# A second batch of column copies in every second step, a tenth row fetch, and column sides loaded slot by slot

## The chip, the cores and the metric

The kernel runs on one core of a Trainium2 chip. The core has a tensor engine (PE, with its weight loads shown as PEld), a vector engine (DVE), a scalar engine (ACT), GpSimd (POOL), and SyncE (SP), which here only issues transfers. Each engine works through its own queue of instructions in order; semaphores make one engine wait for another or for a transfer. A queue also holds register loads, register arithmetic and the issuing of DMAs, which the profile does not count as busy time of the engine.

The metric is the time of one execution on the device in microseconds (us). The kernel before took 1935.29 us, the median of six runs from 1933.59 to 1936.26.

## The reference, cut to what matters

One layer of a graph network over 12500 nodes of 64 features and 200000 edges, which are sorted by their target node, and a layer norm at the end. All of it is float32.

```python
nodes = x[edges].reshape(E, -1)                          # source row and target row of each edge
gates = ssp(edge_attr @ We1 + be1) @ We2 + be2           # ssp(v) = softplus(v) - log 2
gates = gates * (1 - sigmoid(5 * (distance - 3.5)))
h = ssp(nodes @ Wn1 + bn1) @ Wn2 + bn2
sums = zeros_like(x).at[dst].add(h * gates)
new = x + (ssp(sums @ Ws1 + bs1) @ Ws2 + bs2)
out = layernorm(x + new)
```

The source rows `x[src]` are in random order. 

## The kernel before, in words

**Steps and chunks.** The edges are cut into 391 steps of 512 edges, and each step into four chunks of 128. Every chunk needs the source rows of its 128 edges. Since the edges are sorted by target, the targets of 256 edges lie within 42 consecutive nodes, so the target side is not gathered: a table `x @ Wn1[64:] + bn1`, made in the preparation, is read in windows of 42 rows (line 313) and multiplied with a one-hot matrix of the targets (line 342).

**Three ways for the source rows.** 
- GpSimd gathers a chunk with one indirect DMA (line 258), 14 steps ahead of its use. This is the usual way.
- A few chunks, the "row slots", are fetched row by row on ACT's queue: `read_rows` (line 272) loads eight row addresses into registers with one register load, and `fetch` (line 284) issues one small DMA of 256 bytes per row, `ROWS[1]` = 9 rows per step. `slots_by_rows` gives a slot each time 128 rows have come together. In the step of such a slot, DVE also copies the one-hot columns to the row tile (line 345).
- A few chunks, the "column slots", are copied by DVE from `xh`, a transposed copy of x in SBUF with the two halves of the nodes on the two halves of the partitions. `columns` (lines 319 to 337) loads eight column numbers into registers (line 325) and copies eight columns of 128x1 (line 332), once per step from step 8 on. When 128 columns are together, an instruction at line 336 keeps of each column the half that holds the node, by comparing `sides` (the source numbers, broadcast to all partitions, with a sign by partition) with `border`. PE multiplies the result with `wn1_twice` into z (line 383). `slots_by_columns` gives a slot each time 128 columns have come together, and `gather` leaves these chunks out, with a memset by DVE (line 256) in their place.

**One step of the loop** (line 697 on). The order in each queue is the order of the program text; no scheduler changes it. PE: transposes of the gathered chunks (L356), first-layer biases (L368, L407), the scatter of an older step (L436), the edge part of layer 1 (L373), the node part (L380, L383), layer 2 of the step before (L414, L419). ACT: copy of the transposed rows (xT, L363), the register load (L272), three row fetches (L284), exp (L394), three fetches, the logarithm (L397), three fetches. DVE: register load of two window bases (L444), two additions into `sums` (L453), h and msg (L428, L432), softplus (L402), the one-hot matrix of a later step (L342), and the batch of columns (L325, L332). SP: loads of edge features (L305) and windows of the table (L313), five steps ahead.

**Node blocks.** When all edges of 512 nodes are done, a block of the last part (the second network and the layer norm) is spread over the following steps. There are 25 blocks. Low node numbers have more edges, so the first blocks come about 40 steps apart and the last ones 8.

**Preparation.** The first 80 us bring in the inputs, make the table and the register lists. SP loads the sides for all 23 slots in one broadcast of 1.5 MB (line 564), and DVE multiplies them with the sign (line 664).

Of the kernel before, what the change touches and what calls it, by code (L numbers as in the profile page):

```python
# [42 lines left out]
F32 = mybir.dt.float32  # L43
BF16 = mybir.dt.bfloat16
I32 = mybir.dt.int32
U8 = mybir.dt.uint8
AF = mybir.ActivationFunctionType
OP = mybir.AluOpType
# [9 lines left out]
P = 128  # L58
# [14 lines left out]


BLOCK_STEPS = ((2, 3, 4, 4, 6, 7, 8, 9, 10, 14), (2, 3, 3, 4, 5, 6, 7, 8, 9, 10), (1, 2, 1, 2, 3))
ROWS = (0, 9)
READ = 8
ROWS_FROM = -1
READY = (5, 7)
# [1 line left out]
COLUMNS = 8  # L81
COLUMNS_FROM = 8
# [39 lines left out]
def slots_by_columns(NG):  # L122

    slots = []
    for g in range(NG - 2):
        if (g - 3 - COLUMNS_FROM + 1) * COLUMNS >= (len(slots) + 1) * P:
            slots.append((g, 1))
    return slots

# [13 lines left out]
def gnn_resnorm_kernel(ctx: ExitStack, tc: tile.TileContext, a: dict, out: bass.AP, E: int):  # L143
    nc = tc.nc
# [59 lines left out]
    half_n = a["xh"].shape[1]  # L204
    by_columns = {slot: n for n, slot in enumerate(slots_by_columns(NG))}
    columns_i = const.tile([P, column_columns(NG)], I32, name="columns_i")
    sides_i = const.tile([P, len(by_columns) * P], I32, name="sides_i")
    sides = sides_i.bitcast(F32)
    sign = const.tile([P, 1], F32, name="sign")
    border = const.tile([P, 1], F32, name="border")  # L210
    wn1_twice = const.tile([P, 2 * D], F32, name="wn1_twice")
# [64 lines left out]
    def fetch(i, queue, count):  # L276

        for _ in range(min(count, rows_left(queue)) if i >= ROWS_FROM else 0):
            n, r = divmod(fetched[queue], P)
            n += firsts[queue]  # L280
            _, g, k = slots[n]
            if r == 0:
                row_tiles[n, "in"], xrs[g, k] = row_tile(queue, n), row_tile(queue, n)
            ins = queues[queue].dma_start(row_tiles[n, "in"][r : r + 1, :D].bitcast(U8),  # L284
                                          x_bytes[:, bass.ds(row_at[queue].pop(0), 4 * D)])
            tc.no_tile_sem_insts.add(ins.ins.name)
            ins.then_inc(arrived(g, k)[0], 16)
            if r == 0:
                behind(ins, ("rows read", n - 2))
            fetched[queue] += 1  # L290
# [23 lines left out]
                wns[D:DW, g % REST, h, :].bitcast(U8),  # L314
                table_bytes[:, bass.ds(bases[g][h], 8 * D * W)].rearrange("o (w f) -> (o w) f", w=W))), old)

    column_tiles, chosen_columns, columns_done = {}, {}, [0]

    def columns(i, pool):

        n = columns_done[0]
        if i < COLUMNS_FROM or n >= len(by_columns) * P:
            return
        p, q = (n // COLUMNS) % P, n // (COLUMNS * P) * COLUMNS
        _, at = nc.values_load_multi_w_load_instructions(  # L325
            columns_i[p : p + 1, q : q + COLUMNS], engines=[DVE], min_val=0, max_val=half_n - 1,
            skip_runtime_bounds_check_because="src holds rows of x")
        slot = list(by_columns)[n // P]
        if n % P == 0:
            column_tiles[slot] = pool.tile([P, P], F32, name="column", bufs=1)  # L330
        for j in range(COLUMNS):
            nc.vector.tensor_copy(column_tiles[slot][:, n % P + j : n % P + j + 1], xh[:, bass.ds(at[j], 1)])  # L332
        columns_done[0] += COLUMNS
        if columns_done[0] % P == 0:
            chosen_columns[slot] = pool.tile([P, P], F32, name="chosen", bufs=1)
            nc.vector.scalar_tensor_tensor(chosen_columns[slot], sides[:, n // P * P : (n // P + 1) * P], border,
                                           column_tiles[slot], OP.is_ge, OP.mult)

    xTs, zs, us, ss, ghs, hs, msgs, scs = ({} for _ in range(8))

# [202 lines left out]
    with tc.manual_schedule():  # L543
# [4 lines left out]
        with tc.tile_pool(name="prep", bufs=1) as prep:  # L548
# [12 lines left out]
                load_x(i)  # L561
            nc.sync.dma_start(rows_i, a["rows"])
            nc.sync.dma_start(columns_i, a["columns"])
            nc.sync.dma_start(sides_i, a["sides"].partition_broadcast(P))
            dist = cut.rearrange("p g k -> p (g k)")
            nc.sync.dma_start(dist, a["dist_l"])
            dst_i = rel.bitcast(I32)
# [78 lines left out]
            for i in range(PARTS):  # L646
                for c in range(i * CP, (i + 1) * CP, CP // 2):
                    m = CP // 2
                    ps = z_tile().rearrange("p b (k f) -> p (b k) f", k=K)
                    for k in range(m):  # L650
                        nc.tensor.matmul(ps[:, k, :], xT[:, c + k, :], wnb, start=True, stop=True)
                    tb = prep.tile([P, m, 2 * D], F32, name="tb", bufs=6)
                    nc.scalar.copy(tb[:, :K, :], ps[:, :K, :])
                    nc.vector.tensor_copy(tb[:, K:, :], ps[:, K:m, :])
                    nc.sync.dma_start(by_node[:, c : c + m], tb)
                    nc.vector.memset(sums[:, c * P : WIDE if c + m == NCH else (c + m) * P], 0.0)
                if i == 1:
                    nc.vector.tensor_copy(base_i[:1], base_b[:1])
                    nc.vector.tensor_scalar(base_i[32:33], base_b[32:33], float(8 * D), None, OP.mult)
                    nc.vector.tensor_scalar(rows_i, rows_i, float(4 * D), None, OP.mult)  # L660
                    upper = prep.tile([P, column_columns(NG)], F32, name="upper")
                    nc.vector.tensor_scalar(upper, columns_i, float(half_n), float(-half_n), OP.is_ge, OP.mult)
                    nc.vector.tensor_tensor(columns_i, columns_i, upper, OP.add)
                    nc.vector.tensor_scalar(sides, sides_i, sign, None, OP.mult)
                    for k in range(2):
                        nc.vector.tensor_copy(be3[:, k, :], rows[:, 0, :])
                    for k in range(K):
                        nc.vector.tensor_copy(row3[:, :, k, :], rows[:, 1:3, :])
                        nc.vector.tensor_copy(rs3[:, k, :], rows[:, 3, :])
                if i == 2:  # L670
                    nc.scalar.activation(dist, dist, AF.Sigmoid, bias=steep, scale=-5.0)
                    nc.scalar.preload_act_table_set("natural_log_exp_and_others")
                    nc.vector.tensor_copy(rel, dst_i)
                    for t in range(2):
                        r = rel[:, :, 2 * t : 2 * t + 2]
                        nc.vector.tensor_sub(r, r, base_b[:, :NH].rearrange("p (g h) -> p g h", h=2))


        with tc.tile_pool(name="finish", bufs=1) as finish:
# [17 lines left out]
            for i in range(-1, last - 1):  # L697
                now = parts.pop(i, [])
                early = [part for part in now if part.tensor]
                at(load, i + LOADS)  # L700
                if 0 <= i < XH_PARTS:
                    part = slice(half_n * i // XH_PARTS, half_n * (i + 1) // XH_PARTS)
                    nc.sync.dma_start(xh[:, part], a["xh"][:, part])
                if i >= 0:
                    at(gather, i + AHEAD)
                transposes(i + 1, ("load", i + 1), ("gather", i + 1), ("onehot", i + 1))
                xcopy(i + 1)
                read_rows(i, 1, ROWS[1])
                fetch(i, 1, ROWS[1] - 6)
                layer1_bias(i + 1)  # L710
                at(layer2_bias, i)
                for n, g in enumerate(behind_by(i)):
                    scatter(g, zs[i + 1][:, 1, HE + 2 * n * W : HE + 2 * (n + 1) * W])
                layer1_edge(i + 1)
                layer1_node(i + 1)
                exps(i + 1)
                fetch(i, 1, 3)
                logs(i + 1)
                fetch(i, 1, 3)
                for g in behind_by(i):  # L720
                    window(g)
                at(layer2, i)
                for part in early:
                    part.tensor(tx_tile())
                at(hcut, i)
                at(message, i)
                softplus(i + 1)
                for part in early:
                    part.others()
                at(onehot, i + 3)  # L730
                columns(i, finish)
                for part in now:
                    if not part.tensor:
                        part.others()
                complete = i
                if blocks and complete >= blocks[0][1] - PREPARE and not begun:
                    begun = node_block(*blocks[0][0], finish)
                    begun.pop(0).others()
                if blocks and complete >= blocks[0][1]:
                    steps = next(steps for steps in BLOCK_STEPS if i + steps[-1] < last - 1)  # L740
                    for n, part in zip(steps, begun):
                        parts.setdefault(i + n, []).append(part)
                    rest = begun[len(steps) :]
                    blocks.pop(0)
                    begun = None
# [202 lines left out]
```

## Time and profile before

| what | value |
|---|---|
| median of six runs | 1935.29 us |
| profiled execution | 1933.19 us, span 1931.4 us |
| granted clock of PE, mean over the span | 0.983 |
| busy share PE / DVE / ACT / POOL | 92% / 67% / 50% / 74% |
| gathers on POOL (L258) | 1514, mean 0.949 us, the last starts at 1901.6 us |
| row fetches on ACT's queue (L284) | 3328 issues, median 0.223 us each |
| register loads for them (L272) | 416, median 0.742 us |
| column copies on DVE (L332) | 2944, mean 0.148 us |
| register loads for them (L325) | 368, median 0.624 us |
| register loads of window bases (L444) | 391, median 0.543 us |
| copies xT, one per step (L363) | 391, from 80.2 to 1906.1 us |

How to read it: a busy share is the time in which the engine computes, or, for POOL, prepares an indirect DMA. The time that a queue spends on register loads (TENSOR_LOAD), register arithmetic (FUSED_REGOPS) or on issuing (lines with ACTq, SPq, DVEq) is not in it, so an engine that is half idle can have a full queue. The releaser behind an arrow is inferred from semaphores: "issue" means that nothing the profile shows was waited for.

### The profile page before, as it was taken

What the parts mean: (1) busy time and instruction counts of PE and PEld (TensorE: products, weight loads), DVE (VectorE), ACT (ScalarE), POOL (GpSimd) and SP (SyncE); (2) the same over time, 40 slices, a digit from 0 to 9 for tenths busy, and PEclk for the clock granted to TensorE, in tenths of its full rate; (3) what the DMA queues carried; (4) which work ended last, traced back from release to release, by engine and by line L of the source; (5) the groups of instructions that cost most, each with busy time, mean ns of one, the idle gap of its engine ahead of it and who ended that gap; (6) DMA issues with size and microseconds to landing.
All of it is one profiled execution on the core that took longest, in us unless ns stands there. A gap on an engine that the chain in (4) does not pass through costs nothing.

```text
span 1931.4 us, 48239 instructions
## 1 busy us (share of the span) xinstructions
PE 1774.8 (92%) x11419; PEld 1454.7 (75%) x11419; DVE 1299.6 (67%) x5743; ACT 964.8 (50%) x1318; POOL 1437.5 (74%) x1518
## 2 busy tenths in 40 slices
PE   4899999999999999998999998999999999999996
PEld 3787887877787777777777777777777777777775
DVE  4367776777776666666667666676766677677664
ACT  1255555555555454544554554545555555555553
POOL 7777777777777777777777777777777777777773
PEclk9999999999999999999999999999999999999997
DMA  8723332323232232223232232322232223233221
GB/s 231 246 72 72 71 71 67 72 66 73 66 74 68 64 70 64 70 65 70 64 70 66 68 70 66 71 69 67 70 71 68 69 70 71 69 73 73 69 66 24
DMA packets 146498, 147.57 MB, mean 76 GB/s; under 512 B 46735, under 2 KB 93371, under 8 KB 146082
## 3 DMA queue, kind: packets, MB, share of 16 engines
q1 hardware_dynamic: 89578, 92.27, 16.5%
q0 software_dynamic: 48448, 49.71, 14.1%
q10 hardware_dynamic: 8184, 2.44, 0.7%
q8 instruction: 97, 1.59, 0.4%
q14 instruction: 191, 1.56, 0.3%
HBM read 134.61 MB, written 9.63 MB: 75 GB/s over the span
## 4 chain that ended last, share of the span: by engine, by line
PE 45%; ACTq 16%; issue 9%; DVE 9%; DMA 8%; ACT 7%; POOL 3%; DVEq 2%; SPq 1%; POOLq 0%
ACTq L284 13%; PE z L380 10%; PE gh L419 7%; PE z L436 6%; PE tx L356 6%; DMA xg<-in_x,src_i 6%; PE z L373 5%; PE gh L414 4%; ACT xT L363 3%; POOL xg L258 3%; ACT u L394 2%; ACTq L272 2%; PE gh L407 2%; DVE h L428 2%; PE z L368 2%
## 5 line engine op out<-in xcount | busy, mean ns | idle before, releaser
L258 POOL DMA_INDIRECT xg<-in_x,src_i x1514 | 1437.3, 949 | 464.8 <-issue 336.7
L394 ACT ACTIVATE u<-z 128x768 f32<-128x768 f32 x392 | 317.4, 810 | 691.3 <-PE z L380 598.0
L453 DVE TENSOR_TENSOR sums<-sums,z 64x42 f32 x778 | 153.0, 197 | 495.6 <-ACT u L394 453.9
L380 PE MATMUL z<-xT,wns 106*128 106x256 f32 x1564 | 422.1, 393 | 8.4 <-ACT xT L363 7.8
L397 ACT ACTIVATE u<-u,one 128x768 f32<-128x768 f32 x392 | 366.1, 934 | 67.8 <-ACT u L394 63.2
L419 PE MATMUL gh<-consts,s 128*128 128x64 f32 x3128 | 394.9, 269 | 0.0
L419 PEld LDWEIGHTS gh<-consts,s 128*128 128x128 f32 x3128 | 384.1, 193 | 0.0
L402 DVE SCALAR_TENSOR_TENSOR s<-u,z 128x768 f32<-128x768 f32 x392 | 369.3, 942 | 12.2 <-ACT u L397 10.3
L380 PEld LDWEIGHTS z<-xT,wns 106*128 106x128 f32 x1564 | 297.7, 195 | 74.6 <-ACT xT L363 28.4
L356 PE MATMUL tx<-consts,xg 128*106 128x128 f32 x1538 | 238.8, 276 | 93.3 <-DVE h L428 27.5
L436 PEld LDWEIGHTS z<-xg,msg 128*128 128x128 f32 x1556 | 204.6, 191 | 123.8 <-issue 121.1
L363 ACT COPY xT<-tx 106x512 f32<-106x512 f32 x391 | 228.2, 584 | 125.8 <-PE tx L356 115.6
L332 DVE COPY column<-xh 128x1 f32 x2944 | 266.5, 148 | 25.7 <-issue 24.5
L436 PE MATMUL z<-xg,msg 128*128 128x84 f32 x1556 | 264.8, 293 | 0.3
L414 PEld LDWEIGHTS gh<-consts,s 128*128 128x128 f32 x1564 | 239.3, 196 | 31.6 <-DVE s L402 11.1
L356 PEld LDWEIGHTS tx<-consts,xg 128*106 128x106 f32 x1538 | 170.6, 139 | 112.6 <-issue 51.8
L373 PE MATMUL z<-eT,consts 128*128 128x256 f32 x782 | 255.1, 409 | 0.0
L414 PE MATMUL gh<-consts,s 128*128 128x128 f32 x1564 | 244.9, 279 | 4.5 <-DVE s L402 3.8
L428 DVE TENSOR_TENSOR h<-gh,cut 128x256 f32<-128x256 f32 x391 | 166.0, 425 | 26.9 <-PE gh L419 13.9
L432 DVE TENSOR_TENSOR msg<-gh,h 128x256 f32<-128x256 f32 x391 | 165.9, 424 | 13.4
L407 PE MATMUL gh<-row,ones 3*128 3x512 bf16 x391 | 146.8, 375 | 0.0
L342 DVE TENSOR_TENSOR xg<-consts,rel 128x168 f32<-128x168 f32 x391 | 128.3, 328 | 0.0
(102 smaller groups left out, 726.2 us busy)
## 6 DMA issues: line engine op xcount, KB each, us to landing
xr<-in_x ACTq DMA_DIRECT2D x3328, 0.2 KB
eT<-in_eT SPq DMA_DIRECT2D x195, 256.0 KB
xg<-in_x,src_i POOLq DMA_INDIRECT x1514
wns<-table SPq DMA_DIRECT2D x782, 21.0 KB
table<-tb SPq DMA_DIRECT2D x14, 448.0 KB
sums<-in_xT SPq DMA_DIRECT2D x7, 455.0 KB
y<-in_x SPq DMA_DIRECT2D x24, 128.0 KB
out<-y SPq DMA_DIRECT2D x24, 128.0 KB
```

Of the source, the lines that this page charges most:

```text
L258: note(("gather", g), nc.gpsimd.indirect_dma_start(out=xg[:, k, :D], out_offset=None, in_=x, in_offset=bass.IndirectOffsetOnAxis(ap=src_i[ ...
L332: nc.vector.tensor_copy(column_tiles[slot][:, n % P + j : n % P + j + 1], xh[:, bass.ds(at[j], 1)])
L356: ins = nc.tensor.transpose(tx[:, k, :], xgs[g][:, k, :DW], ident)
L363: note(("xcopy", g), nc.scalar.copy(xT, xTs[g]))
L373: nc.tensor.matmul(zs[g][:, 0, :HE], we1.rearrange("a h d -> a (h d)"), eTs[g], start=False, stop=True, skip_group_check=True)
L380: nc.tensor.matmul(zn, wns[:, g % REST, h, :], xTs[g][:, h], start=True, stop=not chosen, skip_group_check=True)
L394: nc.scalar.activation(us[g][:, part], z_of(g)[:, part], AF.Exp)
L397: nc.scalar.activation(us[g][:, part], us[g][:, part], AF.Ln, bias=one)
L402: nc.vector.scalar_tensor_tensor(ss[g].rearrange("p i t e -> p (i t e)")[:, part], us[g][:, part], BIG, z_of(g)[:, part], OP.min, OP.max)
L414: nc.tensor.matmul(v[:, 0, t], ss[g][:, 0, t, :], we2, start=False, stop=False, skip_group_check=True)
L419: nc.tensor.matmul(ghs[g][:, 1, 2 * t + h, :], ss[g][:, 1 + h, t, :], wn2, start=False, stop=h == 1 and t == 1, skip_group_check=True)
L436: ins = nc.tensor.matmul(sc, msgs[g][:, 2 * t : 2 * t + 2, :].rearrange("p h f -> p (h f)"), xgs[g][:, 2 * t : 2 * t + 2, D:DW], start=t = ...
```

## The change

- `ROWS` becomes (0, 10): ten rows are fetched per step on ACT's queue. Behind xT there are three as before (`ROWS[1] - 6` is now written 3), behind exp three, and behind the logarithm four.
- `columns` is called twice in steps with an odd number and once in the others. `slots_by_columns` counts one and a half batches per step.
- The sides are no longer loaded and signed in the preparation. At the first column of each slot SP loads the 128 source numbers of that slot, broadcast to 128 partitions. At the slot's end DVE makes a mask from them in one instruction (times sign, compared with border), and multiplies the columns with it in a second one, in place of the one instruction at line 336. The tiles of side, mask and column have one buffer each.

```diff
-ROWS = (0, 9)
+ROWS = (0, 10)
...
     for g in range(NG - 2):
-        if (g - 3 - COLUMNS_FROM + 1) * COLUMNS >= (len(slots) + 1) * P:
+        steps = g - 3 - COLUMNS_FROM + 1
+        if (steps + steps // 2) * COLUMNS >= (len(slots) + 1) * P:
             slots.append((g, 1))
...
-    sides_i = const.tile([P, len(by_columns) * P], I32, name="sides_i")
-    sides = sides_i.bitcast(F32)
...
         if n % P == 0:
             column_tiles[slot] = pool.tile([P, P], F32, name="column", bufs=1)
+            side_tiles[slot] = pool.tile([P, P], I32, name="side", bufs=1)
+            nc.sync.dma_start(side_tiles[slot], a["sides"][n : n + P].partition_broadcast(P))
...
         if columns_done[0] % P == 0:
+            mask = pool.tile([P, P], F32, name="mask", bufs=1)
+            nc.vector.tensor_scalar(mask, side_tiles[slot], sign, border, OP.mult, OP.is_ge)
             chosen_columns[slot] = pool.tile([P, P], F32, name="chosen", bufs=1)
-            nc.vector.scalar_tensor_tensor(chosen_columns[slot], sides[:, n // P * P : (n // P + 1) * P], border,
-                                           column_tiles[slot], OP.is_ge, OP.mult)
+            nc.vector.tensor_mul(chosen_columns[slot], mask, column_tiles[slot])
...
-            nc.sync.dma_start(sides_i, a["sides"].partition_broadcast(P))
...
-                    nc.vector.tensor_scalar(sides, sides_i, sign, None, OP.mult)
...
-                fetch(i, 1, ROWS[1] - 6)
+                fetch(i, 1, 3)
...
                 fetch(i, 1, 3)
                 logs(i + 1)
-                fetch(i, 1, 3)
+                fetch(i, 1, 4)
...
-                columns(i, finish)
+                for _ in range(1 + i % 2):
+                    columns(i, finish)
```

More of the change, by code (lines that the diff above doesn't have):

```diff
@@ L315, in load @@
                 table_bytes[:, bass.ds(bases[g][h], 8 * D * W)].rearrange("o (w f) -> (o w) f", w=W))), old)
-    column_tiles, chosen_columns, columns_done = {}, {}, [0]
+    column_tiles, side_tiles, chosen_columns, columns_done = {}, {}, {}, [0]
     def columns(i, pool):
```

## The prediction

> **What bounds the kernel now.** The profiled execution took 1933.19 us, of which the span is 1931.4, so 1.8 lie outside; the median of the six runs is 1935.29, 2.1 above it. The sums below are made on the span and get these 3.9 us at the end. 0.2% (3.9 us) is about the least change that a measurement of this kernel can tell.
>
> I read the page's busy shares first. PE at 92% looks like the bound, so I asked the waits whether any engine never waits for work, and found GpSimd.
>
> ```profile
> PE 1774.8 (92%) x11419; PEld 1454.7 (75%) x11419; DVE 1299.6 (67%) x5743; ACT 964.8 (50%) x1318; POOL 1437.5 (74%) x1518
> POOL xg L258 <- issue: 336.7, 1104, 0.3
> ```
>
> GpSimd's longest wait under "issue" is 0.3 us. Its timeline shows the same 0.94 us of work and 0.30 us of pause whatever the pause is put down to, also where it names a DMA or PE:
>
> ```profile
> 1004.18 0.95 POOL L258 DMA_INDIRECT xg<-in_x,src_i  x1 [0.30 <-DMA xg<-in_x,src_i]
> 1005.44 0.94 POOL L258 DMA_INDIRECT xg<-in_x,src_i  x1 [0.30 <-issue]
> 1006.68 0.94 POOL L258 DMA_INDIRECT xg<-in_x,src_i  x1 [0.30 <-PE tx L356]
> ```
>
> So a gather costs 1.249 us, and 1514 of them fill 3.3 to 1902.6 us: 1891 us, with under 9 us of longer pauses, most in preparation. GpSimd sets the end. The other engines catch up with its 14 steps of lead by about 600 us. From there a step takes 4.83 us on average; before, 4.22 to 4.36. So I ask of those early steps what the others need when gathers are not late. By stretches of time, PE is full early and not later:
>
> ```profile
> 200.00:300.00 100.00, 99.00 (x670) 80.53 (x669) 71.30 (x340) 55.38 (x71) 75.60 (x81) 1.00 0.30 71
> 1100.00:1300.00 200.00, 183.99 (x1192) 150.83 (x1190) 139.14 (x621) 101.35 (x139) 151.19 (x161) 0.98 0.30 69
> ```
>
> ScalarE's timeline there, issues (ACTq) between computing instructions, one step per xT copy:
>
> ```profile
> 215.45 0.59 ACT L363 COPY xT<-tx 106x512 f32<-106x512 f32 x1
> 216.39 1.08 ACTq L284 DMA_DIRECT2D xr<-in_x  x3
> 217.58 0.81 ACT L394 ACTIVATE u<-z 128x768 f32<-128x768 f32 x1 [1.54 <-PE z L380]
> 217.65 0.85 ACTq L284 DMA_DIRECT2D xr<-in_x  x3
> 218.55 0.94 ACT L397 ACTIVATE u<-u,one 128x768 f32<-128x768 f32 x1 [0.16 <-ACT u L394]
> 218.62 0.85 ACTq L284 DMA_DIRECT2D xr<-in_x  x3
> 219.51 0.59 ACT L363 COPY xT<-tx 106x512 f32<-106x512 f32 x1
> ```
>
> The reader should see that the queue is full though the engine is half idle: 0.94 us after xT begins (a register load) the issues start, exp follows the third, the logarithm follows the sixth 0.05 us later, and the ninth ends at 219.47, as the logarithm does at 219.49; xT starts at once. The step is 4.06 to 4.09 us, and nothing in it is spare. A step with two register loads took 4.75 (219.51 to 224.26).
>
> DVE, in steps where it was late and hence ran without waiting:
>
> ```profile
> 417.18 0.41 DVE L453 TENSOR_TENSOR sums<-sums,z 64x42 f32 x2 [0.83 <-ACT u L397]
> 417.62 0.42 DVE L428 TENSOR_TENSOR h<-gh,cut 128x256 f32<-128x256 f32 x1
> ...
> 418.42 0.94 DVE L402 SCALAR_TENSOR_TENSOR s<-u,z 128x768 f32<-128x768 f32 x1
> 419.28 0.33 DVE L342 TENSOR_TENSOR xg<-consts,rel 128x168 f32<-128x168 f32 x1
> 419.53 0.64 DVE L332 COPY column<-xh 128x1 f32 x8
> 421.00 0.41 DVE L453 TENSOR_TENSOR sums<-sums,z 64x42 f32 x2 [0.83 <-ACT u L394]
> ```
>
> The idle 0.83 us before L453, named for ACT, is DVE's own queue reading window bases (exp had ended at 420.53). The register loads, by stretches, are slow for list rows 64 to 127 of each 128:
>
> ```profile
> L325 DVEq TENSOR_LOAD <-columns_i x63: 593/609/629, 131.3 to 396.3; - x63
> L444 DVEq TENSOR_LOAD <-base_i x64: 526/537/545, 129.1 to 398.1; - x64
> L325 DVEq TENSOR_LOAD <-columns_i x64: 811/828/849, 400.7 to 682.9; - x64
> L444 DVEq TENSOR_LOAD <-base_i x64: 750/756/774, 402.5 to 686.0; - x64
> ```
>
> **The change part by part.**
>
> GpSimd. The two slot rules give 26 row slots and 23 column slots now, 29 and 35 after. 15 gathers go: 15 x 1.249 = 18.7 us off its chain. That is the most the change can save; it counts only if the steps keep up. From the first xT (80.2) to the last (1906.1 - 18.7), 390 steps would have to average 4.63 us.
>
> ScalarE. The tenth issue stands behind the logarithm, whose cover the three there already use up. Issues are 0.31 us apart ((0.85 - 0.22) / 2), so xT starts 0.31 later in each step: queued behind it are the next register load and every issue, and PE's z waits for xT. Step: 4.08 + 0.31 = 4.39. Register loads bring eight rows: 416 loads in 370 steps now, 464 in 371 after, so 93 steps have two, at 4.75 - 4.08 = 0.67 more. 371 x 4.39 + 93 x 0.67 = 1691 us, 4.56 per step. Node blocks add on ScalarE 0.41 + 0.51 + 0.41 + 0.30 + 0.21 (L491, L492, L511, L519, L520) and 0.6 of idle before them: 2.45 a block, 24 blocks, 59 us, 0.15 per step.
>
> The Perfetto Trace Analysis page of the Trainium skill, DMA Optimizations, says that where descriptor generation binds, balancing DMAs over the issuing engines may help. By that alone the sum would be GpSimd's, about 1917 us. The ACT rows above decide against it: the queue that receives the work has no room.
>
> DVE. Every odd step gets a second register load and eight copies, with nothing to hide behind: load 0.61 or 0.83, eight dispatches at 0.115 ((0.96 - 0.15) / 7 in the row at 1008.97 us), 0.08 between: 1.61 in fast stretches, 1.83 in slow. Queued behind are the window bases, L453, h, msg and the softplus that PE's L414 needs.
> - Slow stretches: a step without waiting took 3.82 (417.18 to 421.00) and 3.71 next, mean 3.77. Two steps: 2 x 3.77 + 1.83 = 9.37, 4.68 per step, above ScalarE's 4.56. Other ends: 4.12, the distance of two L402 at 1002.62 and 1006.74 where the loads were less hidden, giving 5.04; and nothing at all, if the second batch hides. I take 4.68, from the steps in which DVE was late, as it will be.
> - Fast stretches: 3.5 (218.42 - 214.35 less 0.57 spare), two steps 8.61, 4.31 per step, under ScalarE's. The odd step is 0.72 late against 4.39; a late softplus is felt only through L414, xT and exp two steps on. At 414.33 it was 1.5 late and cost 0.50 in xT (the wait on PE at 417.35), so 1.0 was spare at 4.09 a step, more at 4.39. Cost nothing here; without that cover, 0.72 every second step.
> - Also: node blocks 4.1 us of DVE each, 0.25 per step; 29 row slots at about 1.0 (L345 keeps the load from hiding), 0.08; 35 slot ends with a mask and a product for L336's 0.35, at most 0.5 each, 0.05. Slow step in all: 4.68 + 0.38 = 5.06. Fast step: ScalarE's 4.56 + 0.15, rounded up for DVE's sum (4.31 + 0.38 = 4.69, almost equal) to 4.75.
>
> Does the doubled copying hold up GpSimd? In preparation a gather took 1.84 us beside the conversion at L664; in the loop beside copies it is 0.94 to 0.95. The page SBUF — State Buffer of the Trainium skill, section SBUF: two separate sides, says that a fp32 copy within SBUF can lock GpSimd out and starve its gathers. Were that so for each of 1536 added copies at 0.145, GpSimd would lose 223 us and end the run near 2140; the loop's rows speak against it. The new mask is a conversion like L664's, but 35 of at most 0.5 us are hidden, as GpSimd will lead.
>
> SP and PE. The broadcast of sides (1.5 MB) leaves the start, where L664's 1.68 us is on the chain; between 1.7 and 6.4 (1.5 MB at 235 GB/s), I take 2. In the loop SP issues 35 transfers of 64 KB, 0.43 each, and each waits for the mask before it; behind it stand the loads of step i+6, needed five steps (20 us) later and landing in 2. Without that lead it would be 35 x 2 = 70 us. Twelve slots more cost PE 12 x 0.55 at L383, in the 0.3 us a step that PE gains as ScalarE slows.
>
> Sum. Loop start 80.2 - 2 = 78.2; filling, as now, 5 (the first 26 steps average 4.41, the next 4.22); 8 steps before the columns at 4.4, 35; 560 batches of eight in 373 steps, half fast, 187 x 4.75 = 888, half slow, 186 x 5.06 = 941; 10 last steps at 4.3, 43; after the last xT 25.3. Span 2016, with 3.9: 2020 us.
>
> **The rivals.**
> - ScalarE alone is the bound, DVE's second batch hides. For it: DVE is busy 67% only. Against: the 0.83 us pauses that are its queue. 78.2 + 5 + 1691 + 20 steps at 4.15 (83) + 59 + 25.3 + 3.9 = 1945 us.
> - DVE loads hide as little as at 1002.62 (5.04 for 4.68): 186 x 0.36 = 67 more, 2087 us.
> - Faster: GpSimd stays the bound. That needs steps of 4.63; ScalarE alone is at 4.56 + 0.15, so its tenth row must cost under 0.23, not 0.31, and DVE nothing. 1935.3 - 18.7 = 1917 us. For it: all 1514 gathers run without a stall, and ScalarE misses by only 0.08.
> - The change does what it says: both lists follow from the two rules, so this is no case.
>
> **How the numbers follow.** Forecast 0.50, ScalarE alone 0.26, poorly hidden loads 0.17, faster 0.04; 0.03 for the tenth row half hidden, which ends within 0.2% of now. Slower is 0.93. The range goes from ScalarE alone, 1945, to the poorly hidden loads, 2087; beyond it lie faster, same and the outer edges of the two.
>
> **What would show it.** Right: GpSimd's gathers pause for longer than 0.3 us and end well before the others; xT starts 0.3 us after the logarithm's end; odd steps show two groups of eight copies about 0.9 us apart, and DVE, not a gather, ends PE's waits, most in slow stretches. Wrong: gathers back to back up to the end (GpSimd still binds), or a step length that does not differ between slow and fast stretches (then DVE hides).

## The result and the profile after

The changed kernel took 2061.24 us in the median of 16 runs (2042.75 to 2083.74), against 1934.66 of 36 runs of the kernel before. The ratio, taken without the two longest executions, which count as a slower state, is 1.064, with an interval of 1.0625 to 1.0658: 124 us slower (the medians are 127 apart). The forecast was 2020 us, 85 slower, with a range of 1945 to 2087. In the changed kernel's code the same lines carry other numbers: gather L257, xT L365, exp L396, logarithm L399, softplus L404, `sums` L455, the copies L333, layer 2 L416 and L421, the first matmul of a node block L474 (L472 before).

The busy shares and GpSimd's longest waits, of the changed kernel's page and its table of waits (waited for: us in total, times, longest):

```profile
PE 1854.4 (90%) x11443; PEld 1453.8 (70%) x11443; DVE 1468.1 (71%) x7340; ACT 963.7 (47%) x1318; POOL 1425.1 (69%) x1503
POOL xg L257 <- issue: 350.8, 1149, 0.6
POOL xg L257 <- PE z L438: 72.6, 52, 5.6
```

GpSimd, which paused for 0.3 us between its gathers before, now waits up to 5.6 us at a time, by the profile for PE's scatter, which frees the gather buffers, and its last gather starts at 1959.6 us of a span of 2062.1. It no longer sets the end.

ScalarE's timeline of two steps, cut (start, duration, instruction), and two of its waits:

```profile
328.05 0.59 ACT L365 COPY xT<-tx 106x512 f32<-106x512 f32 x1 [0.34 <-issue]
...
331.17 0.94 ACT L399 ACTIVATE u<-u,one 128x768 f32<-128x768 f32 x1 [0.16 <-ACT u L396]
331.25 1.16 ACTq L283 DMA_DIRECT2D xr<-in_x  x4
332.51 0.59 ACT L365 COPY xT<-tx 106x512 f32<-106x512 f32 x1 [0.40 <-PE tx L358]
...
335.85 0.94 ACT L399 ACTIVATE u<-u,one 128x768 f32<-128x768 f32 x1 [0.16 <-ACT u L396]
335.92 1.16 ACTq L283 DMA_DIRECT2D xr<-in_x  x4
337.12 0.59 ACT L365 COPY xT<-tx 106x512 f32<-106x512 f32 x1 [0.34 <-issue]
```

```profile
ACT xT L365 <- PE tx L358: 143.3, 110, 7.5
ACT xT L365 <- issue: 65.4, 181, 0.7
```

In the second step the four issues behind the logarithm end at 337.08, 0.29 us after the logarithm (336.79), and xT starts only then. That is the forecast's 0.31. In the first step the issues end 0.30 us after the logarithm too (332.41 and 332.11), but xT is put down to PE's transposes. Over the whole run xT waited for its own queue in 181 steps (9 in the kernel before) and for the transposes in 110, so ScalarE's queue is not the only one that sets the step.

DVE's timeline of the same two steps:

```profile
328.24 0.41 DVE L455 TENSOR_TENSOR sums<-sums,z 64x42 f32 x2 [0.84 <-ACT u L399]
...
330.65 0.56 DVE L333 COPY column<-xh 128x1 f32 x8
332.04 0.41 DVE L455 TENSOR_TENSOR sums<-sums,z 64x42 f32 x2 [0.83 <-issue]
...
334.39 0.60 DVE L333 COPY column<-xh 128x1 f32 x8
335.63 0.96 DVE L333 COPY column<-xh 128x1 f32 x8 [0.64 <-issue]
337.42 0.41 DVE L455 TENSOR_TENSOR sums<-sums,z 64x42 f32 x2 [0.83 <-ACT u L399]
```

A step with one batch takes 3.80 us, one with two 5.38: 9.18 for the two, where the forecast had 9.37. The second batch shows its pause of 0.64 us for the register load, and its eight copies take 0.96 us, as I read it because they come at the pace of the queue and not behind other work.

The lines that the forecast did not have are PE's: two of its waits, with the same two in the kernel before (L414, L472), then a stretch of its timeline, with the node part (L380) of a step of the kernel before, then busy times in that stretch by engine with the granted clock, the last column but two:

```profile
PE gh L416 <- DVE s L404: 83.9, 103, 2.5
PE tx L474 <- DVE sums L455: 30.6, 20, 3.4
PE gh L414 <- DVE s L402: 3.8, 6, 1.7
PE tx L472 <- DVE sums L453: 9.4, 15, 1.6
```

```profile
343.25 1.19 PE L474 MATMUL tx<-sums,consts 128*128 128x256 f32 x2 [2.04 <-DVE sums L455]
...
347.84 1.91 PE L382 MATMUL z<-xT,wns 106*128 106x256 f32 x4
```

```profile
418.65 1.03 PE L380 MATMUL z<-xT,wns 106*128 106x256 f32 x4
```

```profile
342.00:359.00 17.00, 15.75 (x55) 12.45 (x55) 8.06 (x40) 5.02 (x8) 12.82 (x14) 0.50 0.23 49
```

PE waits 84 us in all for a late softplus, where it waited 4 before. Of 118 us that PE waits for DVE in the loop, 77 fall in the stretches of slow register loads. In the stretch shown PE stood for 2.04 us because a node block's first matmul reads the sums to which a late DVE adds; the clock record goes to half at 342.1, within this pause, and stays there for 17 us, and L382, 1.03 us in the kernel before, took 1.91. Apart from the tail, the clock record has 140 us at half in this execution, in 15 stretches of 3.4 to 17.1 us; the kernel before has 48, in 14 stretches of 3.4. Ahead of each stretch, in the 3.4 us before it, PE had been idle for 1.4 to 2.5 us here and for 0.7 to 1.6 in the kernel before.

The reverse can be counted too. The changes of the clock record lie on a grid of 3.41 us. In the loop of the changed kernel, eight windows of this grid at full clock held 1.6 us or more of idle PE, and half clock followed all eight; of the 503 windows that it did not follow, the longest idle is 1.58 us, and 8 reach the 1.36 us of the least of the 14 that it followed. In the kernel before the two kinds are less apart: 39 of 490 windows that half clock did not follow reach the 0.73 us of the least that it did. So idleness goes ahead of the half clock, but its length alone does not decide.

To weigh this I cut each trace into steps, from one xT to the next, for the steps 10 to 384, and set apart those that a half-clock stretch touches:

| kernel | touched steps, mean | other steps, mean | of these in stretches of fast / slow column loads |
|---|---|---|---|
| before | 14, 5.93 us | 361, 4.63 us | 4.60 / 4.66 |
| changed | 30, 7.58 us | 345, 4.82 us | 4.77 / 4.88 |

The 30 touched steps took 227.5 us, 83 more than 30 of the others. That includes the stalls of PE that fall in them, and a node block's first matmul in 7 of them (16 of the others have one and take 6.2 us). All steps of the changed kernel, touched or not, average 4.93 us in stretches of fast column loads and 5.17 in stretches of slow column loads.

### The profile page after: what moved, and what is told of

Its sections match the earlier page's. It is cut to its first block, busy times and chain, and to the rows that moved or that the text cites. A ratio compares the mean times of both kernels' runs of the same rounds, so it can differ in the third digit from the quotient of the medians.

```text
span 2062.1 us, 52378 instructions
## 1 busy us (share of the span) xinstructions
PE 1854.4 (90%) x11443; PEld 1453.8 (70%) x11443; DVE 1468.1 (71%) x7340; ACT 963.7 (47%) x1318; POOL 1425.1 (69%) x1503
## 4 chain that ended last, share of the span: by engine, by line
PE 23%; DVE 22%; ACTq 16%; issue 15%; DVEq 11%; ACT 6%; DMA 3%; POOL 3%; SPq 0%; POOLq 0%
ACTq L283 14%; DVE column L333 7%; DVEq L324 6%; PE z L382 5%; PE gh L421 4%; DVE h L430 4%; DVEq L446 3%; POOL xg L257 3%; DVE s L404 3%; ACT xT L365 3%; PE gh L416 3%; DVE sums L455 3%; PE z L438 2%; ACTq L271 2%; PE tx L358 2%
## 5 line engine op out<-in xcount | busy, mean ns | idle before, releaser
L257 POOL DMA_INDIRECT xg<-in_x,src_i x1499 | 1424.9, 951 | 535.2 <-issue 350.8
L396 ACT ACTIVATE u<-z 128x768 f32<-128x768 f32 x392 | 317.3, 810 | 712.0 <-PE z L382 453.7
L333 DVE COPY column<-xh 128x1 f32 x4480 | 424.0, 148 | 142.1 <-issue 134.0
L382 PE MATMUL z<-xT,wns 106*128 106x256 f32 x1564 | 438.3, 404 | 43.8 <-ACT xT L365 39.9
L421 PE MATMUL gh<-consts,s 128*128 128x64 f32 x3128 | 403.6, 273 | 0.0
L382 PEld LDWEIGHTS z<-xT,wns 106*128 106x128 f32 x1564 | 287.9, 196 | 156.9 <-ACT xT L365 119.2
L399 ACT ACTIVATE u<-u,one 128x768 f32<-128x768 f32 x392 | 366.0, 934 | 65.0 <-ACT u L396 58.9
L421 PEld LDWEIGHTS gh<-consts,s 128*128 128x128 f32 x3128 | 393.3, 197 | 0.1
L455 DVE TENSOR_TENSOR sums<-sums,z 64x42 f32 x778 | 153.0, 197 | 334.0 <-ACT u L396 163.9
L404 DVE SCALAR_TENSOR_TENSOR s<-u,z 128x768 f32<-128x768 f32 x392 | 369.2, 942 | 11.7 <-ACT u L399 10.4
L416 PE MATMUL gh<-consts,s 128*128 128x128 f32 x1564 | 261.7, 291 | 88.2 <-DVE s L404 83.9
L416 PEld LDWEIGHTS gh<-consts,s 128*128 128x128 f32 x1564 | 230.6, 197 | 155.5 <-DVE s L404 135.6
L365 ACT COPY xT<-tx 106x512 f32<-106x512 f32 x391 | 228.0, 583 | 222.0 <-PE tx L358 143.3
L438 PEld LDWEIGHTS z<-xg,msg 128*128 128x128 f32 x1556 | 209.2, 195 | 131.1 <-issue 124.7
L438 PE MATMUL z<-xg,msg 128*128 128x84 f32 x1556 | 269.9, 297 | 2.4 <-DVE msg L434 2.0
L358 PE MATMUL tx<-consts,xg 128*106 128x128 f32 x1535 | 243.2, 279 | 7.0 <-DMA wns<-table 7.0
L358 PEld LDWEIGHTS tx<-consts,xg 128*106 128x106 f32 x1535 | 185.3, 148 | 11.3 <-issue 8.7
```

What stands on the lines that cost most here:

```text
L257: note(("gather", g), nc.gpsimd.indirect_dma_start(out=xg[:, k, :D], out_offset=None, in_=x, in_offset=bass.IndirectOffsetOnAxis(ap=src_i[ ...
L358: ins = nc.tensor.transpose(tx[:, k, :], xgs[g][:, k, :DW], ident)
L365: note(("xcopy", g), nc.scalar.copy(xT, xTs[g]))
L382: nc.tensor.matmul(zn, wns[:, g % REST, h, :], xTs[g][:, h], start=True, stop=not chosen, skip_group_check=True)
L396: nc.scalar.activation(us[g][:, part], z_of(g)[:, part], AF.Exp)
L399: nc.scalar.activation(us[g][:, part], us[g][:, part], AF.Ln, bias=one)
```

## The experiments

All comparisons are with runs of the kernel before made beside them on the same chip.

**The parts alone.** Ten rows without the rest:

```diff
-ROWS = (0, 9)
+ROWS = (0, 10)
...
-                fetch(i, 1, ROWS[1] - 6)
+                fetch(i, 1, 3)
...
                 logs(i + 1)
-                fetch(i, 1, 3)
+                fetch(i, 1, 4)
```

> The kernel before with ten rows a step alone (three behind xT, three behind exp, four behind the logarithm), one batch of columns, sides in the preparation. Theory of the forecast: the queue of ScalarE becomes the bound by itself at 4.56 us a step and 0.15 for node blocks, near 1945 us. Rival: the tenth row hides and GpSimd stays the bound, with 3 gathers fewer: 1931 us.

Measured: 1953.69 us, ratio 1.0094 (1.0054 to 1.0134), 19 us slower. ScalarE's timeline in this run:

```profile
215.25 0.59 ACT L363 COPY xT<-tx 106x512 f32<-106x512 f32 x1 [0.34 <-issue]
220.27 0.59 ACT L363 COPY xT<-tx 106x512 f32<-106x512 f32 x1 [0.34 <-issue]
224.68 0.59 ACT L363 COPY xT<-tx 106x512 f32<-106x512 f32 x1 [0.34 <-issue]
```

The second step is a single one, 4.41 us (forecast 4.39); the first has two register loads, 5.02 (forecast 4.39 + 0.67 = 5.06). ACT's queue has 45% of the chain that ended last, for 16% in the kernel before, and the clock is at half for only 14 us of the loop. The tenth row does not hide, and the 3 gathers that it saves do not pay for it.

The second batch and the sides slot by slot, with nine rows:

```diff
 (the changed kernel, with)
-ROWS = (0, 10)
+ROWS = (0, 9)
...
-                fetch(i, 1, 4)
+                fetch(i, 1, 3)
```

> The second batch of columns in odd steps and the sides slot by slot, nine rows a step as before. Theory: DVE's queue is most of the loss; with 4.7 us a fast and 5.06 a slow step it is near 2010 us, at least 1990. Rival (ScalarE's tenth row is most of the loss, the second batch hides): GpSimd binds with 12 gathers fewer, 1920 us, or at most 1945.

Measured: 2013.14 us, ratio 1.0404 (1.0376 to 1.0432), 79 us slower. This is the larger part of the loss, and the second batch does not hide. In its trace 29 steps are touched by the half clock (7.30 us on average) and the others take 4.72.

The sides slot by slot, with one batch and nine rows:

```diff
 (the kernel of the run before, with)
-        steps = g - 3 - COLUMNS_FROM + 1
-        if (steps + steps // 2) * COLUMNS >= (len(slots) + 1) * P:
+        if (g - 3 - COLUMNS_FROM + 1) * COLUMNS >= (len(slots) + 1) * P:
...
-                for _ in range(1 + i % 2):
-                    columns(i, finish)
+                columns(i, finish)
```

> The sides slot by slot alone: 23 transfers in the loop, a mask and a product per slot, and no conversion in the preparation. Theory: GpSimd binds from 3 us on and does not wait for the preparation, so nothing is gained or lost: 1934 to 1936 us. Rival: the shorter preparation counts, 1931 or less; or SP, held up by a mask, delays the loads, 1940 or more.

Measured: 1933.42 us, ratio 0.9997 (0.9987 to 1.0006): no difference. GpSimd starts at 3.3 us and does not wait for the preparation. By the ratios the two larger parts alone cost 18 and 78 us, 96 in all, and together they cost 124. Why they cost more than their sum is not shown.

**Node blocks one step later.**

```diff
-BLOCK_STEPS = ((2, 3, 4, 4, 6, 7, 8, 9, 10, 14), (2, 3, 3, 4, 5, 6, 7, 8, 9, 10), (1, 2, 1, 2, 3))
+BLOCK_STEPS = ((3, 4, 5, 5, 7, 8, 9, 10, 11, 15), (3, 4, 4, 5, 6, 7, 8, 9, 10, 11), (1, 2, 1, 2, 3))
```

> The changed kernel with every part of a node block one step later (3, 4, 5, 5, 7, ... for 2, 3, 4, 4, 6, ...), so that PE's first node-block matmul no longer reads sums that DVE adds to in the same step. Theory (formed from the trace after): in the changed kernel PE stands up to 3 us behind that matmul, and its clock then falls to half for 7 to 17 us; without it the half-clock time of the loop drops from 140 us to under 60 and the kernel takes 2000 to 2030 us. Rival: the loss is the steady price of ScalarE's and DVE's queues, and the half clock is not caused by these stalls: 2050 to 2065 us.

Measured: 2062.78 us, ratio 1.0678 (1.0653 to 1.0704), as the changed kernel. The half-clock time of the loop fell only to 102 us, and 29 steps are still touched. But the edit did not take the wait away. PE's wait ahead of the node blocks in this run:

```profile
PE tx L474 <- DVE sums L455: 31.8, 19, 2.5
```

In the changed kernel it was 30.6 us in 20 waits. Moved by a step, the matmul again waits for an addition to `sums` by a late DVE. So the forecast of 2000 to 2030 us failed, but the run says nothing of what the time would be without this wait; whether it is a main source of the half clock stays open.

**The load of the window bases moved ahead of the columns.** No work is left out.

```diff
+                for g in behind_by(i + 1):
+                    window_bases(g)
                 for _ in range(1 + i % 2):
                     columns(i, finish)
```

> The same kernel as in the run before (the changed one with the load of the window bases ahead of the columns), on another chip if one is given: there the kernel before took 2613 us at a granted clock near 0.82, so that PE was the bound and the queues could not be read. Theory: with the kernel before at 1935 us, DVE's queue loses 0.54 to 0.76 us in a step, ScalarE binds, 1945 to 1980 us. Rival: DVE's queue is not what binds, 2030 us or more.

Measured: 2103.15 us, ratio 1.0815 (1.0727 to 1.0903). By the ratios this is 34 us slower than the changed kernel, and my theory fell with it. DVE's timeline:

```profile
334.73 0.41 DVE L455 TENSOR_TENSOR sums<-sums,z 64x42 f32 x2
...
337.58 0.97 DVE L333 COPY column<-xh 128x1 f32 x8 [0.42 <-issue]
338.55 0.41 DVE L455 TENSOR_TENSOR sums<-sums,z 64x42 f32 x2
...
341.38 0.97 DVE L333 COPY column<-xh 128x1 f32 x8 [0.40 <-issue]
342.99 0.96 DVE L333 COPY column<-xh 128x1 f32 x8 [0.64 <-issue]
343.94 0.41 DVE L455 TENSOR_TENSOR sums<-sums,z 64x42 f32 x2
```

The pause of 0.83 us ahead of L455 is gone, and the copies have it instead: 0.4 us of waiting, and 0.97 in place of 0.56 for the eight, as I read it since they no longer come from a queue that has run ahead. Two steps take 9.21 us, as without the move (9.18). So the pause was not a hole that this other order closes: the same register loads, issues and work take the same time in sum. The steps that the half clock does not touch take 4.80 us, as before the move (4.82). But 47 are touched instead of 30, with 351 us instead of 227. The 125 us that the 47 take over 4.80 each are 42 more than the changed kernel's 83; the two profiled executions, 2098.7 and 2063.9, are 35 apart.

**Time against clock.** Over 18 executions of the changed kernel whose clock is recorded, I put the time against the span times one minus the granted clock, the time lost to it (47 us at a clock of 0.977, 100 us at 0.952). A straight line fits with a correlation of 0.98: 2012 us plus 0.69 us for each us lost. For the later node blocks the four runs give 2009 plus 0.72, for the columns alone 1968 plus 0.73, for the moved load 2029 plus 0.72. Without the two longest executions the changed kernel's line is 2015 plus 0.63. Such a line is not the price of the clock by itself: what makes PE stand also takes time. A PE at half clock for 2 us loses 1 us of full clock, so the clock by itself costs at most 1 us for each us lost; with the ten rows alone (five runs) the slope is 1.7. The kernel before shows little of it: 14 runs of it, beside the parts alone, have clocks from 0.974 to 0.980, 12 us apart in time lost, and lie within 3.6 us (1932.6 to 1936.2), where 0.69 would make 8; their line has a slope of 0.13 and a correlation of 0.45. There GpSimd sets the end.

**Runs on disturbed chips.** Seven further runs were made beside a kernel before that itself took 2613, 2659 or 2665 us, at a clock of 0.82 to 0.86, and in the first trace of the moved load the loop began at 145 us instead of 76. What disturbed the chips is open; the chip of the 2659 us is the one on which the kernel before had taken 1934 beside the parts alone. In the traces of these runs PE has 60% or more of the chain that ended last, for 23% in the changed kernel's trace above, with 840 us or more at half clock in the loop. But leaving out the two with an added matmul, steps without half clock take 6.0 to 6.1 us there as well, and xT waits 179 to 226 us for something that the profile does not name. So these runs say nothing of the queues as they are on an undisturbed chip. One was the moved load, told of above from its second run:

> The changed kernel with the register load of the window bases moved: DVE reads the bases for the next step ahead of the columns, behind the softplus and the one-hot matrix, which are still running, in place of behind the columns, where it stood idle for 0.83 us. No work is left out. Theory: DVE's queue loses up to 0.54 to 0.76 us in every step and ScalarE binds as with the ten rows alone: 1945 to 1980 us. Rival: DVE's queue is not what binds, or the load only moves its pause to the columns: 2030 us or more.

Measured: ratio 1.0112 (1.0067 to 1.0157). The others were three kernels that were never seen on an undisturbed chip. One lets the second batch use the registers of the first, and so leaves its register load out:

```diff
-        _, at = nc.values_load_multi_w_load_instructions(
+        if i not in loaded:
+            loaded[i] = nc.values_load_multi_w_load_instructions(
...
+        at = loaded[i]
```

> The changed kernel, but the second batch of an odd step uses the registers of the first, so it copies the first batch's columns again (its output leaves the right columns of half the batches out). It takes 0.61 or 0.83 us of register load from DVE's queue in each odd step, 0.72 x 187 = 135 us, and leaves all copies. Theory: DVE's queue is the bound, the load is part of its price, and with it gone ScalarE's queue binds: 1955 to 1990 us. Rival: the copies or the half clock are the price: 2030 us or more.

> The changed kernel whose second batch of an odd step uses the registers of the first, so that it copies the first batch's columns again (the right columns of half the batches are left out). Theory, after the moved load showed that DVE's queue is bound by the sum of its register loads and issues: 187 loads of 0.61 or 0.83 us leave that queue, 135 us, DVE is no longer late, ScalarE binds, and with shorter stalls of PE the half clock shrinks too: 1955 to 1985 us. Rival: the doubled copies alone keep DVE late: 2020 us or more.

> The changed kernel whose second batch of an odd step uses the registers of the first and copies the first batch's columns again (the right columns of half the batches are left out), alone, in the hope of a chip on which the kernel before takes 1935 us. Theory (DVE's queue is bound by the sum of its loads and issues): 135 us of loads leave it, ScalarE binds, 1955 to 1985 us. Rival (the eight added copies alone keep DVE late, or PE's half clock is the price): 2020 us or more.

Measured: ratios of 1.0083, 1.0087 and 1.0056, in this order. The changed kernel was not measured beside it, so how much of the second batch is its register load stays open. One puts a matmul that nobody needs into each step:

```diff
+                if 0 <= i:
+                    nc.tensor.matmul(zs[i + 1][:, 1, NB - 2 * W :], packed["wnb"], ident[:, : 2 * W], start=True, stop=True,
+                                     skip_group_check=True)
                 at(layer2, i)
```

> The changed kernel with one more fp32 matmul of 84 columns (two passes, about 0.34 us of PE) in each step ahead of layer 2, into a part of z that nobody reads. PE has it free on average (steps of 4.8 us against 4.1 of work). Theory of the clock: PE's idle windows cause the half clock, so its share falls, the granted clock rises, and the time falls by 10 to 40 us although PE has more to do. Rival (the half clock costs nothing, or does not come from idleness): the time stays or rises by up to 0.3 us a step, 2060 to 2170 us.

> The changed kernel with one more fp32 matmul of 84 columns (two passes, about 0.34 us of PE) in each step ahead of layer 2, into a part of z that nobody reads. Theory: PE's idle stretches bring the half clock, which costs 60 to 80 us here; filling them raises the granted clock and takes 10 to 40 us off although PE has more to do. Rival: PE's extra work delays xT and exp, or the half clock is not set by idleness: 2060 us or more, up to 0.34 x 391 = 133 us more.

Measured: ratios of 1.4448 (1.4313 to 1.4583) and 1.4196 (1.4068 to 1.4323), at 3780 and 3807 us. In the first trace the clock is at half for 2657 of 3776 us, and the granted clock 0.65. But the added matmul does not fill PE's pauses: of the 795 us that PE is idle in this trace, 688 lie directly ahead of it. It waits in every step; where the profile names a reason, it is mostly exp or the additions to `sums`, which read the same tile z. So the edit put a wait into each step, and the theory that filling raises the clock was not tested. The last one fetches eight more rows a step on SP's queue, with nothing of the change:

```diff
-ROWS = (0, 9)
+ROWS = (8, 9)
...
+                read_rows(i, 0, ROWS[0])
+                fetch(i, 0, ROWS[0])
                 read_rows(i, 1, ROWS[1])
```

> The kernel before with eight more rows a step fetched on SP's queue, behind its loads (one register load, eight issues at 0.31 us, some 3 us of queue in a step), none of the change. 24 slots more. Theory: GpSimd binds, and 24 gathers at 1.249 go, 30 us: 1905 us. Rival: the loads of the table windows come late behind the rows, or DVE's copies for the row slots bind: 1935 us or more.

Measured: 1.0272 (1.0183 to 1.0362). GpSimd does not set the end there (it waits 409 us for PE's scatter), so fewer gathers cannot help; what it does where GpSimd sets the end is open. No version was found that beats the kernel before.

## Why the prediction was right, and where not

- **GpSimd's 18.7 us** could be had only at 4.63 us a step. The steps take longer and GpSimd waits: right.
- **ScalarE's tenth row**, 0.31 us a step with no cover: right, shown by the row alone (4.41 and 5.02 us for 4.39 and 5.06). The rival "ScalarE alone" was priced at 1945 us; the tenth row alone took 1954.
- **DVE's second batch** as the larger part: right, shown by the second batch alone, 78 us of 124 by the ratios. The sum gave 4.75 us a step where the register loads are fast and 5.06 where they are slow. Steps that the half clock does not touch take 4.77 and 4.88, all steps 4.93 and 5.17. So without the half clock the slow price was too high, and with it both were too low. The two levels differ by 0.11 us, where the forecast had 0.31; the kernel before has 0.06 already. How much of the second batch is its register load and how much its copies was not measured.
- **"Cost nothing here"** for DVE's lateness in fast stretches: the steps without half clock agree (4.77 for 4.75), but the lateness is not free. PE waits 84 us for the softplus and 31 for the sums, and half-clock stretches begin after stalls of PE. The forecast counted only what reaches xT, and the kernel before had shown 4 us of the first wait and 9 of the second.
- **The node blocks** were priced by DVE's and ScalarE's work alone; that PE's L474 waits for sums added in the same step was not seen. The run that moved the blocks by a step left the wait at 32 us, so what it costs is open.
- **The missing term is the half clock, with the stalls that go with it.** The sum had none, because the kernel before loses 0.017 to 0.027 of its clock with little trace in its time. Its size is argued, and two ways to weigh it differ. The line through the 18 runs gives 2012 us at a full clock, and 2018 with the 9.4 us that the tail loses anyway (18.8 us at half), against a forecast of 2020. The median of 2061 us lies on the line at a clock of 0.965, 71.7 us lost, so 0.69 x 62 = 43 us go with the half clock in the loop, near the 39 us between the forecast's rise of 85 and the 124 measured. The table of steps gives 83 us for the touched steps. The others then come out cheaper than in the sum: 375 steps at 4.82 would take 1808 us, where the sum has about 1838. By the table, the forecast came this near partly by luck, since too high a price for the regular steps made up for part of the missing term. Which of the two is nearer is open, as the line takes in more than the clock.
- **Sides**: the sum took 2 us off the start of the loop for the shorter preparation. The first xT came 4.3 us earlier, at 75.9 us. The part alone made no difference, as GpSimd sets the end there; what it gives where GpSimd does not was not measured apart.
- **GpSimd held up by copies**: not seen. A gather's median is 0.944 us in both kernels, with 4480 copies as with 2944.

That an idle PE causes the half clock is argued from what stands ahead of each stretch and from the count of windows; no run here changed idleness alone. The later node blocks left their wait in place, and the added matmul waited itself.

## What to carry to other kernels

Before work is moved off the engine that binds, the queue that receives it has to be added up with its register loads and issues, not by its busy share: ScalarE at 50% and DVE at 67% were full. A pause that is such a load did not go away by another order of the queue; whether fewer loads take it away was not seen. And when an engine in front of PE takes over as the bound, the clock can become part of the price: as long as GpSimd sets the end, half-clock stretches cost little here. With ScalarE's tenth row alone, where no wait of PE in the loop is longer than 1.4 us (1.8 in the kernel before), there was less half clock than before (14 us for 48); with DVE's second batch, where single waits of PE reach 3.2 us, there was more (109). Before an experiment is read, look in its trace whether the wait that it was to remove is gone.

## What was not expected of the hardware

- Stretches of half clock followed 3.4 us in which PE was idle for as little as 0.7 us in the kernel before and 1.4 in the changed one. They lasted 3.4 us in the former and up to 17.1 in the latter. The page TensorE: Matmul & The Clock Gate of the Trainium skill, Part 1: The HAM clock gate, puts the fall to half after a whole idle window of about 3.4 us; here it followed windows in which PE was idle for only part of them.
- The same kernel varied by 2% in time with its clock, from 2043 us at 0.977 to 2084 at 0.952, where the kernel before varied by 0.25%.
- The register loads of DVE come in two durations, 0.61 and 0.83 us, by the half of the partitions in which the list row lies, and the load of the window bases behind them, always from the same partition, changes with them (0.54 and 0.76).
